# A four-layer graph network on one core: zero products between the first columns' sums, a column's blocks in another order, small loads later, and one held multiply that reads SBUF

## The chip, the core and the metric

The kernel runs on one core of a Trainium2 chip. The metric is the device time of one execution in microseconds (us). Before the change it is 2249.74 us, the median of three runs (2249.08 to 2251.6). The engines are named as in the profile: PE is TensorE (matmuls), PEld its weight loads, DVE is VectorE, ACT is ScalarE, POOL is GpSimd and SP is SyncE, whose queue issues the large loads.

## The reference, cut to what matters

The inputs are x (4096 x 128) and adj (4096 x 4096, sparse by value but stored dense, 64 MB). Each of four layers makes x = layernorm(x + layer(x, adj)).

```
layer 0:  hw = h @ W;  h_plus = (adj > 0) @ hw;  h_minus = (adj < 0) @ hw
          e_plus  = leaky_relu(h_plus @ a1 + h_minus @ a2)
          scores = where(adj > 0, e_plus, -9e15), and e_minus where adj < 0
          out = (softmax(scores, axis=1) * adj) @ hw
layer 1:  twice: Tx1 = L @ x; Tx2 = 2 (L @ Tx1) - Tx0
          h = elu(x @ W[0] + Tx1 @ W[1] + Tx2 @ W[2] + b)         (L = adj)
layer 2:  C = alpha_src[None] + alpha_dst[:, None];  tau = adj.T * exp(max(0.2 C, C))
          out = einsum(adj.T * tau / sum(tau), h_prime) + bias     (4 heads of 32)
layer 3:  out = h @ W_self + (adj @ h / clip(sum(adj, 1), 1)) @ W_neigh
```

## The kernel before, in words

The adjacency lies in HBM in two tilings, and every layer reads it again: blocks of 512 x 512 (1 MB, tile `chunk`, from in_adjT) and blocks of 256 x 1024 (also 1 MB, from in_adj). NB = 8 is the number of blocks in a column, P = 128, TB = 4 the tiles of 128 rows in a block, IB = 512. Five buffers named `chunk` (pool `ld`, bufs=5) take the loads, issued by SP in order.

**Layer 0** (L263 to L490) uses that adj has no negative entries; a flag (`bad`) checks it and would start a general version (L158) instead. It goes over the columns i = 0 to 7 (L383). In each it takes the eight blocks j in the order of L387 and L388. For each block VectorE makes a 0/1 mask `pos` (L308), TensorE adds four packed 32-column products of it into one PSUM tile `pden` (edge_sums, L345), and ScalarE runs through the block to look for negative entries (`junk`, L403). At the end of a column ScalarE copies the sums to SBUF (`parts`, L421), eight tiny products collect them (columns(), L352), VectorE and ScalarE make exp(e) from them (L423 to L427), and VectorE scales this column's rows of hw by it (L428). Only then can products with these rows run: product() (L357) of block j needs hw of column j, so in column i only the blocks j < i are multiplied at once. The diagonal block is multiplied in the next column, after its second block (diagonal(), L404). The blocks i+1 and i+2 stay in buffers of their own, three of each (`keep1`, `keep2`, pool l0k), and are multiplied three columns later by above() (L372). Blocks further up are loaded a second time (L459). Outside of the part named below a scheduler at compile time orders the instructions of each engine by priority, that is by place in the program, and by what it reckons to be ready. `keep_in_program_order` takes single instructions out of that.

28 products of a zeroed tile with itself (L317) run at the start, while the first loads are on their way. Nine small inputs for later layers are issued by ScalarE at the end of column 2 (later_inputs, L89), and at column 4 the tables made from them (later_constants, L96).

**Layer 1** (L523 to L582) is three passes of products over all 64 blocks; its last pass (L942 to L967) is interleaved by hand with layer 2.

**Layer 2** makes, for a tile of 128 source rows nt and two target blocks or one, `tau` and `tau2` on VectorE and GpSimd and multiplies them on TensorE (L755). A Pass is two target blocks by two heads (passes 0 to 5), or one block by four heads (passes 6 and 7); each has 32 steps, one per nt. A step of a wide pass is: ScalarE copies the row tile from `chunk` to a PSUM tile `a` (L705, which also sums the row); VectorE does two L733 and the first 704 columns of one more multiply (L737); GpSimd does the remaining columns (L738, L739). Passes 0 and 1 share each `a` and are stepped in pairs. While they run there is only one PSUM tile `a`; a second is opened when pass 0 is finished.

From L876 on (manual_schedule) the order on PE, DVE, ACT and POOL is the program's own. Small sequences are generators in the queue `chains`; one(chains) runs the next one to its next `yield`. These are block_end (L608, the end of layer 1 for a block), block_targets (L655, the table `dv` of a block), targets (L708, the tile D of a pass), finish (L764, the division at the end of a pass) and layer3_blocks (L782, the small products of layer 3). In the loop at L972 there are three calls per pair of steps while no layer-3 product is in `pieces`, and two otherwise. The layer-3 product (L813) is cut into pieces, one per matmul; a credit of 2.0 per pair of wide steps (3.4 for narrow ones) says how many run. It begins when the chain reaches start_product. PSUM tiles named `px`, `pp`, `den` and `num` are single buffers.

The softmax here doesn't subtract the row's maximum and nothing guards it: scores larger than these inputs give would overflow.

## Time and profile before

| Stretch, us | What runs | What is busy |
|---|---|---|
| 0 to 88 | layer 0, columns 0 to 2 | DMA 0.95, PE clock 0.81 |
| 88 to 330 | rest of layer 0 | PE 241.95 of 242 |
| 330 to 1090 | layer 1, three passes | PE 759.47 of 760 |
| 1090 to 1449 | layer 1's last pass, with passes 0 and 1 | PE 343.8 of 359 |
| 1449 to 1509 | end of passes 0 and 1 | DVE 45.27 of 60 |
| 1509 to 1947 | passes 2 to 5, layer-3 pieces | DVE 422, POOL 414 of 438 |
| 1947 to 2188 | passes 6 and 7, layer-3 pieces | PE 231, DVE 227 of 241 |
| 2188 to 2247 | end: last block's layer 3, output | PE 47.8 of 59 |

The page gives busy times in tenths for 40 slices of 56 us:

```profile
PE   6899999999999999999999999968999899999997
DVE  5544461000010110000025777779999999999995
PEclk8899999999999999999999999989999999999999
```

Slices 1 and 2 and slices 27 to 29 are those in which PE or its clock drops. A busy PE says only that matmuls were under way, not that it ran at its peak: in the pass stretches the count of matmuls and the waits tell more. In a line of the timeline the columns are the start in us, the duration in us, the engine, the line, the operation, the tiles written and read, the shape and the count, and in brackets the idle time of the engine just before it with what ended it.

### The profile page before, as it was taken

What the parts mean: (1) busy time and instruction counts of PE and PEld (TensorE: products, weight loads), DVE (VectorE), ACT (ScalarE), POOL (GpSimd) and SP (SyncE); (2) the same over time, 40 slices, a digit from 0 to 9 for tenths busy, and PEclk for the clock granted to TensorE, in tenths of its full rate; (3) what the DMA queues carried; (4) which work ended last, traced back from release to release, by engine and by line L of the source; (5) the groups of instructions that cost most, each with busy time, mean ns of one, the idle gap of its engine ahead of it and who ended that gap; (6) DMA issues with size and microseconds to landing.
All of it is one profiled execution on the core that took longest, in us unless ns stands there. A gap on an engine that the chain in (4) does not pass through costs nothing. (4 is left out here: it accounts for less than half of the span.)

```text
span 2247.5 us, 22889 instructions
## 1 busy us (share of the span) xinstructions
PE 2138.4 (95%) x8588; PEld 848.3 (38%) x8588; DVE 1174.6 (52%) x1815; ACT 561.9 (25%) x1016; POOL 854.4 (38%) x539
## 2 busy tenths in 40 slices
PE   6899999999999999999999999968999899999997
PEld 3344444444444444444443333312222222323334
DVE  5544461000010110000025777779999999999995
ACT  6654200000000000000032223234333433332213
POOL 0000000000000000000004766679999899989990
PEclk8899999999999999999999999989999999999999
DMA  9886748888767677778866556514666566645544
GB/s 397 312 301 214 243 168 283 301 302 300 268 237 259 232 243 262 262 264 272 283 228 232 199 196 235 206 57 165 242 231 238 194 244 243 219 140 204 187 169 170
DMA packets 87144, 528.17 MB, mean 235 GB/s; under 512 B 9328, under 2 KB 15472, under 8 KB 25712
## 3 DMA queue, kind: packets, MB, share of 16 engines
q1 hardware_dynamic: 78992, 521.31, 66.1%
q10 hardware_dynamic: 8032, 5.31, 0.8%
q8 instruction: 69, 1.13, 0.2%
q14 instruction: 51, 0.42, 0.1%
HBM read 524.49 MB, written 2.10 MB: 234 GB/s over the span
## 5 line engine op out<-in xcount | busy, mean ns | idle before, releaser
L733 DVE SCALAR_TENSOR_TENSOR tau<-D,es,a 128x1024 f32<-128x1024 f32 (+1 forms) x640 | 646.6, 1059 | 60.0 <-ACT a L705 34.7
L739 POOL TENSOR_TENSOR tau<-tau,chunk 128x1024 f32<-128x1024 f32 x192 | 456.0, 2375 | 14.4 <-DVE tau L733 13.6
L639 POOL TENSOR_TENSOR x<-x,B2R 128x512 f32<-128x512 f32 x8 | 10.2, 1275 | 1162.2 <-PE px L135 1162.2
L755 PE MATMUL num<-tau,hc 128*32 128x512 f32 x2048 | 325.2, 616 | 13.0 <-POOL tau L739 6.1
L755 PE MATMUL den<-tau,cs 128*32 128x512 f32 x2048 | 332.6, 605 | 4.4 <-DVE tau L733 3.0
L831 PE MATMUL pp<-chunk,xT 128*128 128x512 f32 (+1 forms) x488 | 231.6, 604 | 0.9 <-ACT D L721 0.9
L705 ACT ACTIVATE a<-chunk 128x1024 f32<-128x1024 f32 x160 | 164.3, 1027 | 245.0 <-DVE tau L737 206.1
L531 PE MATMUL pacc<-chunk,t 128*128 128x512 f32 x512 | 223.5, 592 | 0.0
L531 PE MATMUL pacc<-chunk,v 128*128 128x512 f32 x512 | 222.5, 592 | 0.0
L531 PE MATMUL pacc<-chunk,x 128*128 128x512 f32 x512 | 221.9, 593 | 0.0
L738 POOL TENSOR_TENSOR tau<-tau,chunk 128x320 f32<-128x320 f32 x192 | 167.2, 871 | 140.4 <-DVE tau L733 80.0
L955 PE MATMUL pp<-chunk,w 128*128 128x512 f32 x448 | 203.5, 598 | 0.8 <-DVE oT L615 0.8
L357 PE MATMUL pacc<-chunk,hw 128*128 128x512 f32 x408 | 195.1, 620 | 0.0
L737 DVE TENSOR_TENSOR tau<-tau,a 128x704 f32<-128x704 f32 x192 | 168.7, 878 | 0.0
L745 POOL TENSOR_TENSOR tau<-tau,chunk 128x1024 f32<-128x1024 f32 x64 | 151.9, 2373 | 1.1
L755 PEld LDWEIGHTS den<-tau,cs 128*32 128x32 f32 x2048 | 79.0, 112 | 179.5 <-issue 102.9
L755 PEld LDWEIGHTS num<-tau,hc 128*32 128x32 f32 x2048 | 60.8, 110 | 219.0 <-issue 115.4
L531 PEld LDWEIGHTS pacc<-chunk,v 128*128 128x128 f32 x512 | 97.2, 190 | 122.0 <-issue 122.0
L531 PEld LDWEIGHTS pacc<-chunk,x 128*128 128x128 f32 x512 | 96.4, 190 | 116.7 <-issue 116.7
L531 PEld LDWEIGHTS pacc<-chunk,t 128*128 128x128 f32 x512 | 96.1, 190 | 115.3 <-issue 115.3
L831 PEld LDWEIGHTS pp<-chunk,xT 128*128 128x128 f32 x488 | 85.7, 189 | 130.3 <-issue 127.6
L578 DVE COPY w<-ptr 128x512 f32<-128x512 f32 x8 | 5.5, 692 | 241.5 <-PE ptr L135 241.5
(215 smaller groups left out, 1668.1 us busy)
## 6 DMA issues: line engine op xcount, KB each, us to landing
chunk<-in_adjT SPq DMA_DIRECT2D x386, 1024.0 KB, 4.8
chunk<-in_adj SPq DMA_DIRECT2D x80, 1024.0 KB, 4.9
chunk<-in_adj SPq DMA_DIRECT2D x32, 512.0 KB, 4.7
keep<-in_adjT SPq DMA_DIRECT2D x13, 1024.0 KB, 7.2
xT<-in_xT ACTq DMA_DIRECT2D x8, 256.0 KB, 6.5
out<-o ACTq DMA_DIRECT2D x7, 256.0 KB, 2.3
W1A<-in_w1a ACTq DMA_DIRECT2D x1, 384.0 KB, 5.7
W1B<-in_w1b ACTq DMA_DIRECT2D x1, 384.0 KB, 6.5
```

Source lines behind the costliest of these rows:

```text
L357: nc.tensor.matmul(p, hw[:, j * TB + k, :], a[:, k, :], start=first and k == 0, stop=last and k == TB - 1)
L531: nc.tensor.matmul(p, stationary(c * TB + k), a[:, k, :], start=n == 0 and k == 0, stop=n == NB - 1 and k == TB - 1)
L639: nc.gpsimd.tensor_tensor(x[:, tb, :], x[:, tb, :], B2R[:, None, :].to_broadcast([P, TB, F]), ALU.add)
L705: nc.scalar.activation(ap, a, AF.Copy, accum_out=deg[:, nt, self.mp:self.mp + 1])
L733: nc.vector.scalar_tensor_tensor(flat(tau[:, q:q + n]), flat(self.D[:, q:q + n]), es[:, nt, head:head + 1], ap, op0=ALU.max, op1=ALU.mult)
L737: nc.vector.tensor_tensor(t2[:, 0:OWN], t[:, 0:OWN], ap[:, 0:OWN], ALU.mult)
L738: nc.gpsimd.tensor_tensor(t2[:, OWN:WB], t[:, OWN:WB], a[:, OWN:WB], ALU.mult)
L739: nc.gpsimd.tensor_tensor(t2[:, WB:2 * WB], t[:, WB:2 * WB], a, ALU.mult)
L745: nc.gpsimd.tensor_tensor(tau2[:, 2:4, :], tau[:, 2:4, :], rep(a, 2), ALU.mult)
L755: nc.tensor.matmul(acc[32 * q:32 * q + 32, :], weights(nt, head, is_den), r[:, q, :], start=nt == 0, stop=nt == NT - 1)
L831: nc.tensor.matmul(p, y[:, c * TB + k, :], a[:, k, lo:lo + n], start=c == blocks[0] and k == 0, stop=end)
L955: nc.tensor.matmul(p, w[:, c * TB + k, :], a[:, k, :], start=c == 0 and k == 0, stop=c == NB - 1 and k == TB - 1)
```

## The change

In layer 0, products of a zeroed weight tile (`nought`) with the mask just made are put on TensorE after each of the last four blocks of column 0 and each block of column 1. They keep TensorE at work while it waits for loads. The order of a column's blocks puts the two kept blocks ahead of block i-1, whose rows are scaled last. The small loads go to SP's queue at the end of column 5, the tables to column 7, and VectorE instead of ScalarE copies `parts` in the first four columns.

For the end of passes 0 and 1: the second multiply of a held pair (pass 1, after layer 1's last product) reads the row tile from SBUF instead of PSUM, so that `a` is free sooner. finish() does both of its transposes before it goes on, for passes 0, 1 and the last one, and layer3_blocks both halves of a block, for the first pair and the last block; the second PSUM tile for this is `pp` or `den`. Pass 3 gets its targets one at a time. block_targets of block 7 moves behind the start of the first layer-3 product.

The diff, cut to its core:

```diff
-            tc.keep_in_program_order(nc.scalar.dma_start(t, src))
+            tc.keep_in_program_order(nc.sync.dma_start(t, src))
...
+            nought = l0.tile([P, P], BF16, name="nought")
+            nc.vector.memset(nought, 0.0)
+            def keep_busy(moving, n):
+                idle = ps_tr.tile([P, IB], F32, name="ptr")
+                for k in range(n):
+                    nc.tensor.matmul(idle, nought, moving(k), start=True, stop=True)
+            keep_busy(lambda k: xp.rearrange("p t c -> p (t c)")[:, 0:IB], 28)
...
-                order = [*range(i + 3, NB), *range(i)]
-                order = order[:5] + list(range(i + 1, min(i + 3, NB))) + order[5:] + [i]
+                order = [*range(i + 3, NB), *range(i - 1), *range(i + 1, min(i + 3, NB)), *range(max(i - 1, 0), i + 1)]
...
                     edge_sums(pe, pos, j, both, n == 0, n == NB - 1)
+                    if i == 1 or i == 0 and n > 3:
+                        keep_busy(lambda k: pos[:, k, :], TB)
...
-                if i == 2:
+                if i == 5:
                     later_inputs()
+                if i == 7:
+                    later_constants(ps_mm, "pmm")
                 if i == 4:
-                    later_constants(ps_mm, "pmm")
...
-                nc.scalar.copy(parts, pe)
+                (nc.vector.tensor_copy if i < 4 else nc.scalar.copy)(parts, pe)
...
-                    size = 2 if self in passes[2:4] else 1
+                    size = 2 if self is passes[2] else 1
...
-                        nc.vector.tensor_tensor(t2[:, 0:OWN], t[:, 0:OWN], ap[:, 0:OWN], ALU.mult)
+                        only = self is passes[1] and layer1_done
+                        nc.vector.tensor_tensor(t2[:, 0:OWN], t[:, 0:OWN], (a if only else ap)[:, 0:OWN], ALU.mult)
...
-                    q = transpose4(ps_x, "px", lambda k: self.nd[:, 1, k * P:(k + 1) * P])
+                    more = (ps_p, "pp") if self in passes[0:2] else (ps_nd, "den") if self is passes[-1] else None
+                    turn = lambda pool, name, i: transpose4(pool, name, lambda k: self.nd[:, i, k * P:(k + 1) * P])
+                    q = turn(ps_x, "px", 1)
+                    if more:
+                        qn = turn(*more, 0)
                     yield
...
+                        pool, name = ((ps_nd, "den") if final else (ps_p, "pp") if blocks[0] == 0 else (ps_x, "px"))
+                        q = (pool if half else ps_x).tile([P, 2, 2, F], F32, name=name if half else "px")
...
+                        if half == 0 and (final or blocks[0] == 0):
+                            continue
                         yield
...
+                            if this is passes[1]:
+                                chains.append(block_targets(NB - 1))
...
-                            chains.append(block_targets(ib))
+                            if ib < NB - 1:
+                                chains.append(block_targets(ib))
...
                 load()
+                layer1_done.append(True)
```

## The prediction

> **What bounds the kernel now.** I read the table of windows by stage first, because the shares of the page average four layers with different limits. Its columns are the stretch in us, then its length, the busy time and count of each engine, the granted TensorE clock, the DMA share and GB/s.
>
> ```profile
> 0.00:88.00 88.00, 63.66 (x286) 30.38 (x286) 50.22 (x117) 58.90 (x66) 0.70 (x6) 0.81 0.95 375
> 88.00:330.00 242.00, 241.95 (x866) 103.94 (x862) 121.37 (x271) 89.51 (x107) 0.00 (x0) 0.99 0.68 236
> 330.00:1090.00 760.00, 759.47 (x1939) 346.86 (x1938) 59.11 (x128) 37.84 (x61) 0.00 (x0) 1.00 0.79 268
> 1449.00:1509.00 60.00, 41.93 (x235) 10.84 (x238) 45.27 (x56) 19.74 (x38) 40.32 (x26) 0.83 0.21 77
> 1509.00:1947.00 438.00, 408.73 (x2402) 120.88 (x2394) 422.24 (x437) 176.31 (x334) 414.07 (x267) 0.98 0.61 222
> ```
>
> From 88 to 1090 us TensorE is never free at full clock, so what makes its solid stretch begin earlier moves all that follows by the same amount. From 1509 on VectorE (422 of 438) and GpSimd (414) run in lockstep. The two holes are 0 to 88 us (clock 0.81, DMA 0.95) and 1449 to 1509 us (no engine over 45 of 60, DMA 0.21). The change edits both.
>
> The timeline shows the first hole's end: how column 2 of layer 0 closes and diagonal(2), the first product of the solid stretch, starts at 88.40.
>
> ```profile
> 78.76 0.83 PE L345 MATMUL pden<-pos,both 128*32 128x512 bf16 x12
> 81.37 0.59 ACT L421 COPY parts<-pden 128x512 f32<-128x512 f32 x1 [4.01 <-DMA W2S<-in_w2T]
> 81.53 0.14 DVE L104 COPY att<-ATS 32x1 f32<-32x1 f32 x1 [4.73 <-DMA ATS<-in_att_src]
> 82.01 1.87 PE L352 MATMUL ptr<-sel,parts 128*128 128x2 f32 x8 [2.41 <-ACT parts L421]
> 87.66 0.68 DVE L428 TENSOR_TENSOR hw<-hw,xe 128x512 f32<-128x512 f32 x1
> ```
>
> The sums end at 79.6, but their copy waits until ScalarE has issued nine small loads, VectorE stands 4.73 us on one of these loads, and TensorE's column sums run at half clock. At full clock the same sums take half:
>
> ```profile
> 111.28 0.95 PE L352 MATMUL ptr<-sel,parts 128*128 128x2 f32 x8
> ```
>
> The waits of 25 to 90 us name the other cost of the half clock: ScalarE, standing in order for a slow diagonal product, frees the load buffers late.
>
> ```profile
> ACT numT L364 <- PE pacc L357: 7.6, 2, 4.3
> DVE e L423 <- PE ptr L352: 9.2, 3, 5.6
> ```
>
> The second hole, in VectorE's timeline: block_targets(7) (L664, L667), then the next pair of steps, which starts only after ScalarE's copy L705.
>
> ```profile
> 1479.84 0.88 DVE L737 TENSOR_TENSOR tau<-tau,a 128x704 f32<-128x704 f32 x1
> 1480.00 2.38 POOL L739 TENSOR_TENSOR tau<-tau,chunk 128x1024 f32<-128x1024 f32 x1
> 1484.69 1.01 ACT L705 ACTIVATE a<-chunk 128x1024 f32<-128x1024 f32 x1
> 1486.01 2.47 DVE L733 SCALAR_TENSOR_TENSOR tau<-D,es,a 128x1024 f32<-128x1024 f32 x2 [1.83 <-ACT a L705]
> 1492.50 1.03 ACT L705 ACTIVATE a<-chunk 128x1024 f32<-128x1024 f32 x1 [6.58 <-DVE tau L737]
> 1493.73 2.47 DVE L733 SCALAR_TENSOR_TENSOR tau<-D,es,a 128x1024 f32<-128x1024 f32 x2 [1.27 <-issue]
> ```
>
> Here ScalarE's copy waits for the last reader of the one PSUM tile `a`, the L737 of the second step, and VectorE idles 1.27 us per pair.
>
> **What the Trainium skill says.** "TensorE: Matmul & The Clock Gate", section "What's actually happening": the array's clock is halved unless the recent activity window (about 3.4 us) was busy. The trace agrees: 0.50 from 30 to 40 us where TensorE works 4.9 of 10, and 1.87 against 0.95 us above. That products of zeros count is shown by the 28 of L317: 0.43 us apart at first, 0.21 us after 6.7 us. "SBUF — State Buffer", section "Who interferes with whom": a VectorE instruction with two SBUF inputs contends with a GpSimd one that reads SBUF, and the later one waits. No L737 of before has two SBUF inputs (`a` is PSUM), so no row shows it. "Trainium Kernel Development and Optimization", section "Key Constraints": issuing loads from another engine only saves the issuer's time. That fits: the loads cost ScalarE 75.36 to 81.33 us.
>
> **The change, part by part: layer 0.** (1) Zeros: 4 products after each of the last 4 blocks of column 0 and all 8 of column 1, 48 in all. At 0.21 us they are 0.86 us per block, 10 us; at half clock 1.7 us per block. A block lands each 2.5 us (1.05 MB at 421 GB/s) and column 1 holds 8 sums of 0.4, two products of 3.4 and 6.9 us of zeros: 17 of 20 us, so all of it lies beside the loads. Queued behind the zeros is the column sum (at most 0.86 us, beside the copy of 0.7). (2) With the clock up, diagonal(0) takes 3.4, not 5.9 us (it starts at 39.68), and ScalarE frees buffers 2 us sooner. (3) Order: for column 2, 5 6 7 0 3 4 1 2 in place of 5 6 7 0 1 3 4 2. The kept blocks have free buffers of their own, so the loads are no longer held at that point. In return the product of block i-1 (3.4 us) stands ahead of the last block's sums on TensorE, up to 1.5 us later than its landing would allow. (4) The nine loads leave ScalarE for SP at column 5, where DMA is 0.66 to 0.77 busy and TensorE is the bound: about 5 us of issue beside five loaded buffers, at nothing. The copies of later_constants move to column 7, where VectorE is half idle. (5) `parts` on VectorE: 0.69 us (the like copy of L548) instead of 0.56 on ScalarE; the masks queue behind it, but ScalarE's copy waited behind 1.91 us activations.
>
> Sum for column 2: the last block landed at 73.0 and should land at 70.5 to 72; sums by 73.5. Column 3 of the trace shows a close without disturbance: copy at 110.23, hw scaled at 115.57, 5.3 us. So hw is ready at 79 instead of 88.34. TensorE may still be cold for diagonal(2) (5.48 us now, no zeros in column 2). From then on the work is the same; I take off 1.5 us for blocks that then land too late (kept buffers that wait for above()). I take 8 us; bounds 2 (only the two waits on the small loads) and 11.
>
> **Layer 2 to 3.** (6) block_targets(7) leaves the hole: pair 28 to 29 took 1474.28 to 1486.01, 11.7 us. Two steps are 6.36 (2.47 + 0.88 less overlap, 3.18 each) plus 0.4 for a copy that starts early: 6.9. That is -4.9. Its instructions run later, among the steps: L664 and L667 (1.4 us) and the 1.23 us between them on VectorE, +2.6. (7) L737 of the second step reads `a` from SBUF: the copy starts 0.88 us earlier in three more pairs (7.7 us each). But GpSimd's L739, ready at the same moment, must now wait out L737: its pair becomes 2 x (0.87 + 2.37) + 0.88 = 7.4 us and replaces VectorE as the bound. I take 0.4 for each, -1.2 (bounds -2.6 and, if VectorE is the one that waits 2.4 us in each of six steps, +9). (8) finish() and layer3_blocks for the first pair do two transposes, or both halves, at a time: four calls of the chain fewer. At three calls per pair of steps the layer-3 product begins 1.3 pairs sooner (now 1552.9), while TensorE is idle (18.6 of 25 us busy at 1520 to 1545). With 2 pieces per pair, 2.7 pieces of 0.86 us leave the end, where leftover pieces still run at 2200.85 to 2204.3 although y is done by 2202.4: -2.3. The eight scalings in one go are 2 us on ScalarE beside its slack of 2.03 us per step: nothing. (9) Pass 3's targets one at a time: two more calls, due 60 us later: nothing. The last pass's wider finish: -0.3.
>
> Sum: -4.9 + 2.6 - 1.2 - 2.3 - 0.3 = -6.1. In all -14.1: 2249.7 - 14.1 = 2236.
>
> **Rivals.** A, the forecast, 0.50. B, layer 0 gives little: column 2's end stays set by landings, and the product ahead of the last sums eats what the loads gain: -3, with -6 from the rest, 2241. For it: DMA is at 1.01 until 55 us. Against: VectorE and ScalarE waits after the landing are most of the 15 us from 73.0 to 88.4. 0.17. C, the lock: VectorE or GpSimd loses in (7) what (6) gained, the rest -8 and -1: 2241. For it: L737 and L739 start 0.16 us apart. Against: L737 starts first in each pair. 0.15. D, slower: the zeros and the later product delay each early column, the masks wait behind `parts` in VectorE's order, layer 0 loses 4 us, and the lock costs 2.4 us in some steps: +5, 2255. For it: the order of layer 0's instructions is chosen ahead of the run, and no row shows the new one. 0.11. E, both holes close: -11 and -9, 2230. 0.07.
>
> **How the numbers follow.** 2236 is A's. The range of 2227 to 2247 holds A, B, C and most of E, and leaves D out. Within 0.2% is 2245.2 to 2254.2. A, E and most of B and C are faster: 0.81; 0.08 for the same; 0.11 slower.
>
> **What would show it.** TensorE's clock at or near 1.0 from 30 to 60 us; diagonal(2) at about 80; layer 1's first product at about 331 instead of 338.9; no L664 between 1440 and 1500 less the shift; the step after pair 28 following at 7 us; the first L831 about 20 us earlier (8 + 4 + 9, the last rounded up); no L831 of block 6 left when y is ready. It is wrong if diagonal(2) starts past 85, if L737 of the second step takes over 0.9 us, or if GpSimd's wait before L739 delays the next L733.

## The result and the profile after

The changed kernel takes 2245.41 us, median of four runs (2242.59 to 2247.08), against 2249.84 us for the kernel before (2249.08 to 2251.6): a ratio of 0.9978, 95% interval 0.9961 to 0.9995. The direction was forecast, the size was not: -4.4 us instead of -14.1, and the time lies in the upper part of the range. The profiled execution is the slowest of the four. Its span is 2245.2 us against 2247.5, so the differences that I follow through the two traces sum to -2.3 us.

Line numbers move by some 5 in layer 0 and by 9 or more later: L345 is now L350, L352 L357, L357 L362, L421 L430, L428 L437, L531 L540, L705 L714, L733 L742, L737 L748, L739 L750, L831 L853, L955 L980.

The table of windows of the kernel after, in the columns of the table before:

```profile
0.00:88.00 88.00, 71.87 (x334) 32.13 (x334) 52.46 (x122) 55.59 (x60) 0.70 (x6) 0.94 0.91 365
88.00:330.00 242.00, 240.93 (x867) 102.14 (x866) 123.23 (x277) 90.86 (x108) 0.00 (x0) 1.00 0.68 242
330.00:1090.00 760.00, 758.38 (x1932) 346.66 (x1931) 57.80 (x122) 37.81 (x61) 0.00 (x0) 1.00 0.78 267
1449.00:1509.00 60.00, 43.25 (x274) 12.66 (x272) 50.87 (x62) 20.57 (x41) 49.02 (x30) 0.89 0.27 93
1509.00:1947.00 438.00, 414.79 (x2376) 119.07 (x2380) 422.75 (x439) 179.60 (x338) 414.36 (x267) 0.99 0.62 223
```

Both holes look better filled: TensorE's clock is 0.94 instead of 0.81 in the first, and VectorE works 50.9 instead of 45.3 us in the second. But the row from 330 to 1090, which the change does not touch, has lost 1.1 us of TensorE's time. A table of busy shares says neither what the filling is worth nor why that row changed; for that I took the start of the same instruction in both traces.

| Start of | before | after | difference |
|---|---|---|---|
| diagonal(2), first L357 / L362 of it | 88.40 | 81.94 | -6.46 |
| last product of layer 0 | 336.98 | 335.45 | -1.53 |
| first product of layer 1 (L531 / L540) | 338.90 | 337.37 | -1.53 |
| last product of layer 1 | 1089.52 | 1090.65 | +1.13 |
| first product of layer 2's interleave (L955 / L980) | 1092.20 | 1094.17 | +1.97 |
| step after pair 28 (L733 / L742) | 1486.0 | 1483.7 | -2.3 |
| first step of pass 2 | 1509.2 | 1504.5 | -4.7 |
| 17th step of pass 2 | 1567.8 | 1566.7 | -1.1 |
| 97th step of passes 2 to 5 | 1841.9 | 1838.3 | -3.6 |
| first step of pass 6 | 1946.8 | 1943.2 | -3.6 |
| last step | 2185.2 | 2183.0 | -2.2 |

So of 6.5 us gained at diagonal(2) 4.9 are gone by the end of layer 0, and 3.5 more are lost at the two ends of layer 1. Layer 2 begins 2 us LATER than before, and all that the change brings is made after that point.

**The first hole.** The timeline after, at the end of column 2:

```profile
77.31 0.40 PE L350 MATMUL pden<-pos,both 128*32 128x512 bf16 x4
77.76 0.69 DVE L430 COPY parts<-pden 128x512 f32<-128x512 f32 x1 [5.47 <-PE pden L350]
78.51 1.05 PE L357 MATMUL ptr<-sel,parts 128*128 128x2 f32 x8 [0.80 <-DVE parts L430]
81.21 0.68 DVE L437 TENSOR_TENSOR hw<-hw,xe 128x512 f32<-128x512 f32 x1
81.94 5.18 PE L362 MATMUL pacc<-chunk,hw 128*128 128x512 f32 x6
```

The chain from the copy to hw takes 3.45 us instead of 6.29, the column sums run at full clock (1.05 against 1.87), but VectorE has stood 5.47 us in front of the copy, waiting for TensorE's last sums. The long waits of the same stretch answer to the two rows of before:

```profile
ACT numT L369 <- PE pacc L362: 7.9, 3, 4.2
DVE e L432 <- PE ptr L357: 2.3, 2, 1.1
```

The wait for the column sums is a quarter of what it was; that of ScalarE for the diagonal product has not moved.

**The second hole**, in the timeline after. The pair begins at 1476.80, the next one at 1483.72:

```profile
1479.18 0.88 DVE L748 TENSOR_TENSOR tau<-tau,a 128x704 f32<-128x704 f32 x1
1479.35 2.38 POOL L750 TENSOR_TENSOR tau<-tau,chunk 128x1024 f32<-128x1024 f32 x1 [0.33 <-DVE tau L742]
1482.37 0.94 DVE L748 TENSOR_TENSOR tau<-tau,chunk 128x704 f32<-128x704 f32 x1
1482.48 1.03 ACT L714 ACTIVATE a<-chunk 128x1024 f32<-128x1024 f32 x1 [6.12 <-DVE tau L742]
1482.53 3.02 POOL L750 TENSOR_TENSOR tau<-tau,chunk 128x1024 f32<-128x1024 f32 x1
1483.72 2.47 DVE L742 SCALAR_TENSOR_TENSOR tau<-D,es,a 128x1024 f32<-128x1024 f32 x2 [0.41 <-issue]
```

ScalarE's copy L714 starts beside the second L748 and no longer behind it, and the pair takes 6.9 us, exactly as forecast for this one pair. The three pairs after it take 6.9 us too, against 7.7 before.

**The start of layer 1.** This is where 2.66 us go. The timeline before, and then that after:

```profile
340.50 0.43 DVE L541 TENSOR_TENSOR wd<-W1B 128x256 f32<-128x256 f32 x1 [1.35 <-DMA W1B<-in_w1b]
344.85 0.49 PE L135 MATMUL ptr<-ident,x 128*128 128x128 f32 x2 [0.53 <-DVE x L149]
```

```profile
340.07 0.43 DVE L550 TENSOR_TENSOR wd<-W1B 128x256 f32<-128x256 f32 x1 [2.44 <-DMA W1B<-in_w1b]
344.41 0.50 PE L135 MATMUL ptr<-ident,x 128*128 128x128 f32 x2 [1.62 <-DVE x L149]
```

The load of the weights W1B landed at 340.48 before and at 340.04 after: it was issued 2.2 us earlier, beside a block of the adjacency with the DMA full (share 1.03 from 335 to 340), and came only 0.44 us earlier. VectorE's difference wd of these weights, which no product needs before 870 us, stands in its order ahead of the last normalization of layer 0; TensorE waits for the transposes that follow. After 1.62 us of waiting TensorE's clock falls to a half, as the windows after show (0.66 is the mean clock of the stretch):

```profile
340.00:345.00 5.00, 3.38 (x13) 1.52 (x12) 4.46 (x22) 0.30 (x1) 0.00 (x0) 1.00 0.73 252
345.00:350.00 5.00, 5.00 (x18) 3.04 (x18) 2.39 (x14) 0.58 (x1) 0.00 (x0) 0.66 0.05 21
```

Before, the wait of 0.53 us at this place left the clock at 1.00. The bill is 1.09 us of wait and 1.57 us of half clock. The second part need not come with every wait of this size: the last section shows longer waits that left the clock alone.

**The end of layer 1** costs 0.84 us more. Before, TensorE went on at once (L955 at 1092.20, no bracket); after, its first product for layer 2 waits for ScalarE's copy out of the PSUM pool of layer 1:

```profile
1094.17 5.42 PE L980 MATMUL pp<-chunk,w 128*128 128x512 f32 x12 [0.68 <-ACT xT L591]
```

### The profile page after: what moved, and what is told of

It reads as the page before. It is cut to its first block, busy times and chain, and to the rows that moved or that the text cites. A ratio compares the mean times of both kernels' runs of the same rounds, so it can differ in the third digit from the quotient of the medians.

```text
span 2245.2 us, 22994 instructions
## 1 busy us (share of the span) xinstructions
PE 2148.4 (96%) x8636; PEld 847.1 (38%) x8636; DVE 1178.2 (52%) x1820; ACT 562.1 (25%) x1014; POOL 857.3 (38%) x539
## 5 line engine op out<-in xcount | busy, mean ns | idle before, releaser
L742 DVE SCALAR_TENSOR_TENSOR tau<-D,es,a 128x1024 f32<-128x1024 f32 (+1 forms) x640 | 646.6, 1059 | 52.3 <-ACT a L714 32.0
L750 POOL TENSOR_TENSOR tau<-tau,chunk 128x1024 f32<-128x1024 f32 x192 | 459.1, 2391 | 12.7 <-DVE tau L742 12.0
L766 PE MATMUL num<-tau,hc 128*32 128x512 f32 x2048 | 332.7, 611 | 13.6 <-POOL tau L750 6.4
L766 PE MATMUL den<-tau,cs 128*32 128x512 f32 x2048 | 338.3, 601 | 2.0 <-DVE tau L742 0.4
L853 PE MATMUL pp<-chunk,xT 128*128 128x512 f32 (+1 forms) x488 | 231.7, 604 | 0.0
L714 ACT ACTIVATE a<-chunk 128x1024 f32<-128x1024 f32 x160 | 164.3, 1027 | 253.0 <-DVE tau L748 194.4
L540 PE MATMUL pacc<-chunk,t 128*128 128x512 f32 x512 | 223.5, 592 | 0.0
L540 PE MATMUL pacc<-chunk,x 128*128 128x512 f32 x512 | 223.1, 595 | 0.0
L540 PE MATMUL pacc<-chunk,v 128*128 128x512 f32 x512 | 222.5, 592 | 0.0
L980 PE MATMUL pp<-chunk,w 128*128 128x512 f32 x448 | 203.6, 598 | 1.5 <-DVE oT L624 0.8
L362 PE MATMUL pacc<-chunk,hw 128*128 128x512 f32 x408 | 194.0, 615 | 1.1 <-DVE hw L437 1.1
L748 DVE TENSOR_TENSOR tau<-tau,a 128x704 f32<-128x704 f32 x186 | 163.4, 879 | 0.0
L540 PEld LDWEIGHTS pacc<-chunk,v 128*128 128x128 f32 x512 | 97.2, 190 | 122.0 <-issue 122.0
L540 PEld LDWEIGHTS pacc<-chunk,x 128*128 128x128 f32 x512 | 96.7, 191 | 117.5 <-issue 117.4
L540 PEld LDWEIGHTS pacc<-chunk,t 128*128 128x128 f32 x512 | 96.1, 190 | 115.3 <-issue 115.3
L853 PEld LDWEIGHTS pp<-chunk,xT 128*128 128x128 f32 x488 | 85.7, 190 | 128.6 <-issue 125.8
```

Source lines behind the costliest of these rows:

```text
L362: nc.tensor.matmul(p, hw[:, j * TB + k, :], a[:, k, :], start=first and k == 0, stop=last and k == TB - 1)
L540: nc.tensor.matmul(p, stationary(c * TB + k), a[:, k, :], start=n == 0 and k == 0, stop=n == NB - 1 and k == TB - 1)
L714: nc.scalar.activation(ap, a, AF.Copy, accum_out=deg[:, nt, self.mp:self.mp + 1])
L742: nc.vector.scalar_tensor_tensor(flat(tau[:, q:q + n]), flat(self.D[:, q:q + n]), es[:, nt, head:head + 1], ap, op0=ALU.max, op1=ALU.mult)
L748: nc.vector.tensor_tensor(t2[:, 0:OWN], t[:, 0:OWN], (a if only else ap)[:, 0:OWN], ALU.mult)
L750: nc.gpsimd.tensor_tensor(t2[:, WB:2 * WB], t[:, WB:2 * WB], a, ALU.mult)
```

## The experiments

All were timed against the kernel before on the same chip. Times differ from run to run by more than most effects here: seven kernels with the same first layer (the change, e1, e3, e4, e10, e11, e12) scaled hw of column 2 at 79.0 to 81.9 us and began layer 1 at 334.5 to 338.1. So I judge each step by starts and waits inside a trace, one for each kernel, and the sum by the ratio. "Relative" means less the shift that the trace already has at layer 2's first product.

### Each half alone (e1, e2)

e1 is the kernel before with the hunks of layer 0 only, e2 that with the hunks of layers 2 and 3 only. Cut to one line for each hunk:

```diff
 # e1
+tc.keep_in_program_order(nc.sync.dma_start(t, src))        # at column 5; constants at column 7
+order = [*range(i + 3, NB), *range(i - 1), *range(i + 1, min(i + 3, NB)), *range(max(i - 1, 0), i + 1)]
+keep_busy(lambda k: pos[:, k, :], TB)
+(nc.vector.tensor_copy if i < 4 else nc.scalar.copy)(parts, pe)
 # e2
+only = self is passes[1] and layer1_done
+more = (ps_p, "pp") if self in passes[0:2] else (ps_nd, "den") if self is passes[-1] else None
+if this is passes[1]: chains.append(block_targets(NB - 1))
```

> The kernel before with the edits of the first layer alone. Theory S (seams): the earlier start of the solid stretch is mostly filled up again by TensorE's own work, so layer 1's first product stands 1.5 us earlier than before; then the wait of VectorE for W1B and the clock after it take 2.7 us, and a new wait of the first product of layer 2 for ScalarE takes 0.9 us. Layer 2 begins 2.1 us LATER than before, the end is 2251.9 (+2.1). Rival A (the forecast's sum with a smaller layer 0): the first layer's edits keep a gain of 1.5 to 2 us, 2248. Rival C (the two halves disturb each other): the first layer's edits alone bring the 8 us forecast, 2242.

> The kernel before with the edits of layers 2 and 3 alone. Theory S: layer 2 begins as before (first step 1194.5), the pair 28 to 29 takes 6.9 us, the three pairs after it 6.9 instead of 7.7, the moved block_targets(7) costs 2.6 later, and nothing is gained at the end: -4.4, 2245.4, as fast as the whole change. Rival A: these edits bring about 3 us and the first layer's about 1.5, 2247. Rival C: 2249 or more, since the head start of 8 us is needed for them.

e1: 2249.36 us, ratio 1.0002 (0.9994 to 1.0011). Diagonal(2) 6.9 us earlier, layer 1's first product 2.0 earlier, its last product 0.1 later, layer 2's first product 0.9 later, the end 1.1 later. TensorE's wait at 343 us was 1.06 instead of 1.62 us here; it lost 2.1 us at that place and 0.84 at the next, where 2.7 and 0.9 were expected. The time is 0.5 us above that of the kernel before, timed with it at 2248.9; theory S said 2.1 above, rival A 1.7 below, rival C some 8 below. That rules out C; between S and A it is the trace that decides, where the head start is used up at layer 1's last product. The first layer's edits alone bring nothing that can be measured.

e2: 2245.43 us, ratio 0.9988 (0.9981 to 0.9994). Layer 2 begins 0.2 us earlier than before, pass 2 7.1 earlier, the end is 4.3 earlier. Half of the change makes all of its gain.

### The wait for W1B (e3) and the one for ScalarE (e4)

```diff
-nc.vector.tensor_sub(wd, W1B[:, 0:HH, :], W1B[:, 2 * HH:3 * HH, :])
-nc.vector.tensor_scalar_mul(w2x, W1B[:, 2 * HH:3 * HH, :], 2.0)
+nc.gpsimd.tensor_tensor(wd, W1B[:, 0:HH, :], W1B[:, 2 * HH:3 * HH, :], ALU.subtract)
+nc.gpsimd.tensor_tensor(w2x, W1B[:, 2 * HH:3 * HH, :], W1B[:, 2 * HH:3 * HH, :], ALU.add)
```

```diff
-ph = ps_mm.tile([P, IB], F32, name="pmm")
+ph = (ps_acc if ib == NB - 1 else ps_mm).tile([P, IB], F32, name="pacc" if ib == NB - 1 else "pmm")
```

> The changed kernel, with wd and w2x made from W1B by GpSimd, which is idle there, instead of VectorE. Theory S: VectorE no longer stands 2.4 us on the load of W1B, TensorE's idle stretch of 1.62 us at 342.8 shrinks to 0.3 us or none, the clock stays at 1.0 from 345 to 350, layer 1 ends 2.7 us earlier than in the changed kernel, and the time is 2242.7. Rival T (throttle): the half clock there comes of the longer unbroken work of TensorE, not of its wait; it stays at 0.66 from 345 to 350, and the time is 2244.5 to 2245.4.

> As the run before, and the last of the products pmm that ScalarE copies to xT at the end of layer 1 is written to a buffer of ps_acc instead of ps_mm, so that the first product of layer 2 has no wait for ScalarE. Theory S: the first product of layer 2 follows at once, 0.9 us more, 2241.8. Rival D (the 0.9 us are needed anyway, for the load of the first block of layer 2 or for w): no difference to the run before, 2242.7.

e3: 2242.7 us, ratio 0.9974 (0.9964 to 0.9985). The windows of e3:

```profile
340.00:345.00 5.00, 5.00 (x25) 3.08 (x24) 2.32 (x11) 0.59 (x1) 0.02 (x1) 1.00 0.60 213
345.00:350.00 5.00, 5.00 (x16) 2.22 (x15) 2.97 (x16) 0.88 (x2) 0.00 (x0) 1.00 0.74 224
```

TensorE has no idle time and full clock. From layer 1's first product to its 33rd the trace gains 0.8 us on the kernel before, where the change lost 2.66. The throttle rival falls: the same amount of work, without the wait, kept its clock, and so did e4 to e15, which all have this edit. The time does not show the step by itself: the intervals of 0.9974 and 0.9978 overlap, and that 2242.7 is the number expected is in part luck, since the kernel before ran at 2248.9 beside it, 0.9 us faster than beside the change. That edit leaves the order of all other instructions of VectorE as it was, so I use e3 as the base of all that follows.

e4: the wait is gone; layer 1's last and layer 2's first product have the same shift (-1.54 each, against -3.32 and -2.48 in e3). Rival D is out for that place. But the run as a whole is not faster, 2244.29 us, ratio 0.9977 (0.9970 to 0.9984): its layer 0 ran 1.8 us later by the scatter named above, and at the last step only 2.8 us of the relative gain are left (e3: 3.6). 0.8 us is shown in the trace and not in the time. Why the wait appears with the edits of layer 0 and not without them (e2 has none) I did not find. The later kernels narrow it: e5 to e15 all have it (3.5 us from the last product of layer 1 to the first of layer 2, against 2.68 before and in e2), with or without the zeros, the new order or the moved loads. Of the edits of layer 0 only `parts` on VectorE is in all of these, and it was not taken out alone.

### The parts of layer 0 (e5 to e8)

All on top of e3. e5 leaves the zeros of columns 0 and 1 out (the 28 products at the start stay), e6 has the old order, e7 the small loads and constants where they were, and e8 has eight more products of zeros:

```diff
 # e5
-if i == 1 or i == 0 and n > 3:
-    keep_busy(lambda k: pos[:, k, :], TB)
 # e6
-order = [*range(i + 3, NB), *range(i - 1), *range(i + 1, min(i + 3, NB)), *range(max(i - 1, 0), i + 1)]
+order = [*range(i + 3, NB), *range(i)]
+order = order[:5] + list(range(i + 1, min(i + 3, NB))) + order[5:] + [i]
 # e7
-tc.keep_in_program_order(nc.sync.dma_start(t, src))
+tc.keep_in_program_order(nc.scalar.dma_start(t, src))
-if i == 5:
+if i == 2:
     later_inputs()
-if i == 7:
+if i == 4:
     later_constants(ps_mm, "pmm")
 # e8
 sums = columns(parts)
+if i == 2:
+    keep_busy(lambda k: pos[:, k % TB, :], 8)
```

> The kernel of the run with wd on GpSimd (2242.7, hw of column 2 at 80.8, first product of layer 1 at 336.35), without the products of zeros of columns 0 and 1. Theory Z (the clock is what brings column 2 early): hw of column 2 at 83 or later, clock 0.5 again from 30 to 40. Rival L (the small loads and the landings are): hw within 1 us of 80.8. For the end, theory F (the time saved at column 2 is filled up again, because TensorE's own sums move into the solid stretch): whatever hw does, layer 1 begins within 1.5 us of 336.35, 2242.7 to 2244; rival G (start decides): layer 1 shifts by as much as hw.

> The kernel of the run with wd on GpSimd, with the old order of a column's blocks. Theory F: hw of column 2 comes later (83 to 86), diagonal(2) with it, but TensorE then has done more sums ahead of it and fewer switches behind it, so that layer 1 begins within 1.5 us of 336.35: 2242 to 2244. Rival G: layer 1 shifts by as much as hw, 2 to 5 us: 2245 to 2248.

> The kernel of the run with wd on GpSimd, with the nine small loads back on ScalarE at column 2 and the copies of later_constants back at column 4. The forecast's step: hw of column 2 waits for ScalarE's issues and for a small load again, and comes at 86 to 87. Theory F: layer 1 begins 1 to 2 us later than 336.35, about 2244. Rival G: 5 to 6 us later, 2248. Rival N (the loads didn't matter): hw at 81, 2242.7.

> The kernel of the run with wd on GpSimd, and eight more products of zeros after the column sums of column 2, where TensorE stands 1.8 us and its clock falls to a half. Theory F: diagonal(2) runs at full clock, 3.7 instead of 5.2 us, and as TensorE is never free after it the whole 1.5 us arrive: 2241.2. Rival H (the loads that follow set the pace after diagonal(2)): a wait of the same size opens later in the layer, 2242.7. Rival I: the zeros stand ahead of the first sums of column 3 and put diagonal(2) off by 1 us or more, 2243.7.

| | hw of column 2 | diagonal(2) to the end of layer 0 | first product of layer 1 | time, us | ratio |
|---|---|---|---|---|---|
| before | 87.66 | 249.2 | 338.90 | 2249.68 | 1 |
| e3 | 80.83 | 253.4 | 336.35 | 2242.70 | 0.9974 (0.9964 to 0.9985) |
| e5 no zeros | 81.27 | 253.5 | 336.80 | 2242.74 | 0.9969 (0.9958 to 0.9981) |
| e6 old order | 78.29 | 253.4 | 333.81 | 2240.41 | 0.9958 (0.9941 to 0.9975) |
| e7 loads back | 82.57 | 250.1 | 334.69 | 2239.50 | 0.9961 (0.9947 to 0.9975) |
| e8 warm | 82.45 | 251.8 | 336.27 | 2240.72 | 0.9964 (0.9952 to 0.9977) |

**e5: with the new order the 48 zeros bring nothing.** Rival L holds: hw and the stretch behind it are as with them. Up to column 2's close the clock was a symptom and not the bound. Since the DMA is full there (share 1.01 to 1.02 from 20 to 50 us), I take the loads to set the pace. One thing did move: the last block of column 2 landed at 71.8 in e5, and at 70.4 to 71.1 in all the runs with the zeros. That is some 1 us, of which hw shows 0.4, because with the new order the sums come late anyway. What the zeros are worth with the old order was not tried.

**e6: the new order is a loss.** It was expected to be a gain ahead of diagonal(2); its removal is one of 2.5 us. The last block of column 2 lands at 70.9 us in both. The timeline after, then that of e6, from the mask of that block (L308) to the copy:

```profile
71.06 1.23 DVE L308 TENSOR_SCALAR pos<-chunk 128x2048 bf16<-128x2048 f32 x1 [1.26 <-DMA chunk<-in_adjT]
73.15 1.98 PE L362 MATMUL pacc<-chunk,hw 128*128 128x512 f32 x4
75.39 1.98 PE L362 MATMUL pacc<-chunk,hw 128*128 128x512 f32 x4
77.76 0.69 DVE L430 COPY parts<-pden 128x512 f32<-128x512 f32 x1 [5.47 <-PE pden L350]
```

```profile
71.00 1.23 DVE L308 TENSOR_SCALAR pos<-chunk 128x2048 bf16<-128x2048 f32 x1 [1.26 <-DMA chunk<-in_adjT]
71.41 2.84 PE L362 MATMUL pacc<-keep,hw 128*128 128x512 f32 x6
74.18 0.62 PE L350 MATMUL pden<-pos,both 128*32 128x512 bf16 x8
74.85 0.69 DVE L430 COPY parts<-pden 128x512 f32<-128x512 f32 x1 [2.62 <-PE pden L350]
```

With the new order the product of block i-1, in two parts of 1.98 us, stands on TensorE ahead of the last sums: VectorE waits 5.47 us, with the old order 2.62. The forecast saw this term and put it at "up to 1.5 us"; the earlier landing that should have paid for it is not there. The scatter is as large as the effect: the copy stands 4.8 to 7.9 us behind the landing with the new order (ten runs, mean 6.4), and 3.6 to 5.0 with the old one in e6, e9, e13 and e15, but 6.4 in e14. With all five the mean is 4.6, so the order costs about 2 us. Why e14 is late I did not trace; the small loads in ScalarE's queue are not the reason by themselves, since e9 has them there too.

**e7: the small loads do hold up column 2, and moving them is not free.** In e7's timeline ScalarE's exponential stands behind the last of its nine issues:

```profile
79.59 0.33 ACTq L94 DMA_DIRECT2D W<-in_w3s  x1
79.97 0.20 ACT L435 ACTIVATE xe<-xe 128x4 f32<-128x4 f32 x1 [4.99 <-DMA W2S<-in_w2T]
80.82 0.13 DVE L104 COPY att<-ATS 32x1 f32<-32x1 f32 x1
82.57 0.69 DVE L436 TENSOR_TENSOR hw<-hw,xe 128x512 f32<-128x512 f32 x1
```

hw is 1.7 us later, as expected in sign (3.4 to 4.4 us less than expected). Yet layer 1 begins 1.7 us EARLIER than in e3, which neither theory F nor G had: the stretch behind diagonal(2) is 3.4 us shorter. So theory F, that the gain is only filled up by TensorE's own sums, is not enough. What the stretch is made of can be counted in the traces. Behind diagonal(2)'s start there are always 464 matmuls of product(). The other terms are below; the column "half clock" says for how long TensorE's granted clock was 0.50 behind diagonal(2)'s start, and the last one takes half of that off the stretch.

| | groups of products | matmuls of sums | TensorE idle, us | half clock, us | stretch, us | at full clock, us |
|---|---|---|---|---|---|---|
| before | 58 | 280 | 0.05 | 3.6 | 249.2 | 247.4 |
| e9 | 60 | 288 | 0.05 | 5.2 | 251.0 | 248.4 |
| e7 | 61 | 288 | 0.05 | 2.8 | 250.1 | 248.7 |
| e14 | 62 | 288 | 1.07 | 3.2 | 251.7 | 250.1 |
| e15 | 63 | 292 | 3.52 | 6.8 | 257.0 | 253.6 |
| change | 66 | 292 | 1.07 | 4.8 | 254.1 | 251.7 |
| e3, e6 | 66 | 292 | 1.07 | 3.4 | 253.4 | 251.7 |
| e8, e13 | 66 | 292 | 1.07 | 0 | 251.8, 251.7 | 251.8, 251.7 |

The last column takes away what looked like scatter: every kernel with 66 groups needs 251.7 or 251.8 us, whatever its order and its zeros. The 0.7 us by which the change's stretch is longer than e3's are half clock.

The time between two matmuls shows what a group costs: product to product 0.43 us, product to sums 0.52, sums to product 0.31, and the second product of a group 0.53; sums that follow sums come in fours at 0.22. A group more costs 0.09 + 0.31 + 0.10, less the 0.22 that its sums would need behind other sums: an estimate of 0.28 us, and eight are 2.3. The idle time at column 3's close is 1.0. Twelve matmuls of sums, three fours or 0.7 us, are work that TensorE did before in its hole, ahead of diagonal(2), and does now behind it. That is 4.0 of the 4.3 us at full clock; the rest I have not traced. The same sum gives e9, e7 and e14 to within 0.1 us (1.0, 1.3 and 2.6 for 1.0, 1.3 and 2.7) and leaves 0.7 us of e15's 6.2 open. "From then on the work is the same" was wrong twice.

**e8: a warm diagonal(2) is worth 1.7 us.** Its stretch is 251.8 instead of 253.4, and the half clock behind diagonal(2) is gone, 3.4 us of it in e3. The run shows no gain at layer 1's start because its column 2 closed 1.6 us later, before the added zeros come into play; e13 settles it.

### Putting the parts together (e9, e13 to e15)

e9 combines e6 and e7. e13 is e3 with the old order, e8's zeros, and layer 3's calls one at a time again (see e12). e14 and e15, both with the old order, take the moved inputs apart:

```diff
 # e14, on e6
-tc.keep_in_program_order(nc.sync.dma_start(t, src))
+tc.keep_in_program_order(nc.scalar.dma_start(t, src))
-if i == 5:
+if i == 2:
     later_inputs()
 # e15, on e6
-tc.keep_in_program_order(nc.sync.dma_start(t, src))
+tc.keep_in_program_order(nc.scalar.dma_start(t, src))
```

> The kernel of the run with wd on GpSimd, with both the old order of a column's blocks and the small inputs back at column 2 (constants at column 4); zeros, parts on VectorE and the edits of layers 2 and 3 stay. Theory K: the order costs 2.5 us ahead of diagonal(2), in TensorE's own order, and the moved inputs cost some 3.5 us behind it, in more switches between products and sums (66 groups of products; this kernel has 60) and one idle stretch. The two are apart, so they add: hw of column 2 at 80 (78.3 + 1.7), the stretch from diagonal(2) to the last product 249 to 249.5 us, first product of layer 1 at 331.5 to 332, 2237 to 2238. Rival M (both come from the same landings): no better than the faster of the two alone, 2239.5 to 2240.5.

> The kernel of the run with wd on GpSimd, with the old order of blocks, eight more products of zeros behind the column sums of column 2, and finish() and layer3_blocks one at a time again. Theory K2: column 2 closes within 4 us of the landing of its last block, diagonal(2) at 79 at full clock, the stretch behind it 251.8 instead of 253.4, first product of layer 1 at 332.2; the step of 8.0 to 9.5 us at 1965 to 1974 is one of 6.0 again; in sum 2237 to 2238.5. Rival M2 (what is saved ahead is lost in later waits): 2240 to 2242.

> The kernel of the run with wd on GpSimd and the old order, with the nine small loads back on ScalarE at column 2 and the constants left at column 7. If the loads' place at column 5 made the stretch behind diagonal(2) longer: 250 to 251 us, and as VectorE has no copy of a small load at column 4, hw of column 2 at 79 to 80: layer 1 at 331 to 332, 2238. If the constants at column 7 did: 253 or more, 2241.

> The kernel of the run with wd on GpSimd and the old order, with the nine small loads at column 5 as in the change, but issued by ScalarE. If SyncE's queue (nine issues ahead of the chunks) made the stretch longer: 250 to 251 us, layer 1 at 330 to 331, 2238. If it is the place in TensorE's order that the loads and constants shift (63 groups of products here, 66 with SyncE): about 252, 2239. If the constants at column 7: 253.4, 2240.4 as with SyncE.

e9: 2242.15 us, ratio 0.9962 (0.9948 to 0.9976), and theory K falls. The parts do not add. `parts` was copied at 74.5, as early as in e6, but hw came at 83.45: with the sums early, the whole wait for the small loads stands open, 8.9 us from copy to hw instead of 3.4. The stretch was 251.0, 1.5 us longer than expected: TensorE waited so long for hw that 5.2 us behind diagonal(2) ran at half clock, against 2.8 in e7. At full clock e9's stretch is the shortest of all the kernels with moved edits, 248.4. So the forecast's step on the small loads was right with the old order (5.5 us), and 1.7 us in e7 because the late sums hid the rest.

e13: 2237.36 us, ratio 0.9950 (0.9936 to 0.9963), 12.6 us faster than before and, by times or by ratios, 8 or 6 faster than the change. Column 2 closed 5.0 us behind the landing (4 expected), diagonal(2) at 80.09 (79 expected), the stretch behind it 251.7 (251.8 expected), layer 1 at 333.16 (332.2 expected), and the time as expected. The timeline of e13:

```profile
77.57 1.89 PE L320 MATMUL ptr<-pos,nought 128*128 128x512 bf16 x7
80.09 2.84 PE L362 MATMUL pacc<-chunk,hw 128*128 128x512 f32 x6 [0.20 <-DVE hw L439]
```

The six matmuls take 2.84 us; after the change they took 5.18. Here the zeros are worth something: TensorE is about to run without a break, and there is no load to hide the cold clock behind.

e14: 2242.53 us, ratio 0.9970 (0.9959 to 0.9981); hw at 82.87, because ScalarE's exponential again waits behind the nine issues, stretch 251.7 with 1.02 us of idle time at 174.6. e15: 2244.35 us, ratio 0.9978 (0.9967 to 0.9988); hw at 77.9, the earliest of all, but a stretch of 257.0, with 3.5 us of idle time, 2.25 of it in one piece at 171.9 where TensorE waits for a mask of VectorE. None of the three expectations for e15 fits: SyncE's queue is not what made the stretch longer, for without it the stretch is worse. At full clock, all with the old order, the stretch is 248.4 with loads and constants where they were (e9), 250.1 with the constants at column 7 (e14), 251.7 with the loads on SyncE at column 5 as well (e6), and 253.6 with these on ScalarE (e15). So the constants' move costs 1.7 us, of which 1.0 is the idle time, and the loads' move 1.6 more, one trace each. Each place gives another order of TensorE's and VectorE's instructions, and with it another count of groups and of waits; why the scheduler chooses these orders stays open.

### The parts of layers 2 and 3 (e10 to e12)

All on top of e3. e10 has L748 read PSUM in every step again, e11 has block_targets(7) back behind the last block, e12 undoes the paired calls of finish() and layer3_blocks (cut to its core):

```diff
 # e10
-nc.vector.tensor_tensor(t2[:, 0:OWN], t[:, 0:OWN], (a if only else ap)[:, 0:OWN], ALU.mult)
+nc.vector.tensor_tensor(t2[:, 0:OWN], t[:, 0:OWN], ap[:, 0:OWN], ALU.mult)
 # e11
-if this is passes[1]:
-    chains.append(block_targets(NB - 1))
-if ib < NB - 1:
-    chains.append(block_targets(ib))
+chains.append(block_targets(ib))
 # e12
-q = turn(ps_x, "px", 1)
-if more:
-    qn = turn(*more, 0)
+q = transpose4(ps_x, "px", lambda k: self.nd[:, 1, k * P:(k + 1) * P])
...
-if half == 0 and (final or blocks[0] == 0):
-    continue
```

> The kernel of the run with wd on GpSimd, with the held pairs' multiply by a (128x704) reading PSUM in every step again. Theory B (the copy of the next pair waits for nothing but that multiply; the lock of VectorE and GpSimd on SBUF costs nothing): the three pairs after the first moved one take 7.7 instead of 6.9 us, step 64 stands 2.4 us later (1502.7), and all of it arrives at the end: 2245. The forecast's size: 1.2 us, 2243.9. Rival Q (given back later, in the lockstep of passes 2 and 3): 2242.7.

> The kernel of the run with wd on GpSimd, with block_targets(7) back behind the last block of layer 2. Theory B and the forecast agree: the pair 28 to 29 takes 11.7 less the 0.8 of the SBUF copy again, 4.8 us more at step 58, of which 2.6 come back where it now runs in passes 2 and 3: 2244.9. Rival Q (the later cost is as large as the gain): 2242.7.

> The kernel of the run with wd on GpSimd, with finish() and layer3_blocks taking one transpose and one half at a time again (and the last pass's wider finish undone). The forecast's step: the product of layer 3 begins some 8 us later, and 2 to 2.7 of its pieces move to the end, 2.3 us, with the last finish 2.6: 2245.3. Theory E (the queue of pieces runs empty between two pairs of blocks, so a head start is lost in that gap): the first product of layer 3 some 8 us later, the gap after its 128th matmul shorter by as much, the end within 0.5 us: 2242.7, and 0.3 for the last finish.

e10: 2246.48 us, ratio 0.9986 (0.9980 to 0.9993), against 0.9974 for e3. In its timeline ScalarE's copy is behind the multiply again, and VectorE waits 1.27 us per pair:

```profile
1483.92 0.88 DVE L746 TENSOR_TENSOR tau<-tau,a 128x704 f32<-128x704 f32 x1
1484.83 1.03 ACT L714 ACTIVATE a<-chunk 128x1024 f32<-128x1024 f32 x1 [6.57 <-DVE tau L746]
1486.07 2.47 DVE L742 SCALAR_TENSOR_TENSOR tau<-D,es,a 128x1024 f32<-128x1024 f32 x2 [1.27 <-issue]
```

The pairs take 7.7 us, pass 2 begins 2.8 us later relative to e3, and at the first step of pass 6 it is 3.2. Theory B holds up to there: more than twice the forecast's 1.2 us. At the last step 1.4 are left, because of one stall: at the 17th step of pass 6 some traces wait 2 us longer than others (the step takes 5.9 us in e3 to e6, e9, e14 and e15, and 3.9 in the change, e2, e7, e8, e10 and e11), which moves the end by some 1.7 us. So a difference of that size at the end says little about an edit.

e11: 2241.48 us, ratio 0.9966 (0.9955 to 0.9978): not slower than e3. Relative to layer 2's start the pair 28 to 29 costs 4.1 us more (4.8 in the expectation); 2.7 are back by the 17th step of pass 2, as the forecast said; but 1.0 more comes back between the 65th and the 97th step of passes 2 to 5, and 0.5 stays at the first step of pass 6. That e11 ends up ahead is the stall just named. Rival Q: the move is right in its mechanism, and worth 0.5 us at most at the end.

e12: 2242.19 us, ratio 0.9970 (0.9958 to 0.9982). The layer-3 product begins 7.7 us later than in e3 (9.6 relative), and nothing is lost by it: in the profiled run the end is 2.6 us earlier than e3's relative to layer 2's start, while the times of e12 and e3 are the same within their intervals. So the forecast's gain is not there. The head start dies in a gap: the product of the first two blocks runs out of pieces before y of the next two is ready. The windows of its matmuls alone (busy time and count on PE and PEld, clock, DMA share, GB/s), before and then after:

```profile
1770.00:1780.00 10.00, 0.00 (x0) 0.00 (x0) 0.83 0.41 154
```

```profile
1750.00:1760.00 10.00, 0.53 (x2) 0.00 (x0) 1.00 0.57 211
1760.00:1770.00 10.00, 0.00 (x0) 0.00 (x0) 0.83 0.61 211
```

Between the 128th and the 129th of these matmuls lie 19.4 us before, 24.6 after, 18.0 in e12. And there is a price, at the seventh step of pass 6. In the timeline after, then in that of e12, VectorE's accumulation of a finished piece:

```profile
1969.08 1.88 PE L853 MATMUL pp<-chunk,xT 128*128 128x512 f32 x4
1971.00 0.69 DVE L862 TENSOR_TENSOR acc<-pp,acc 128x512 f32<-128x512 f32 x1 [3.39 <-PE pp L853]
```

```profile
1960.43 1.02 PE L842 MATMUL pp<-chunk,xT 128*128 128x512 f32 x2
1961.70 0.68 DVE L851 TENSOR_TENSOR acc<-pp,acc 128x512 f32<-128x512 f32 x1
```

With the head start the last pieces of a group fall into that step, four matmuls instead of two stand on TensorE ahead of the accumulation, and the step takes 9.5 us (8.0 in the kernels with e3's edit), before and in e12 and e13 6.0. Part of this comes back in the traces where the stall at the 17th step is missing: that step takes 6.1 us before and 3.9 after. Over eleven traces with the paired calls and all other edits of layers 2 and 3 (the change, e2 to e9, e14 and e15) the relative gain at the last step was 2.8 to 5.6 us, and without the pairs 6.6 (e12) and 6.0 (e13).

## Why the prediction was right or wrong

**Layer 0, -8: the step that failed.** At layer 2's first product it was +2.0 instead. Of the 10 us between them 2.9 were lost ahead of diagonal(2), 3.4 in the stretch behind it, and 3.5 at the two ends of layer 1. Taken apart:

- The close of column 2. hw was to be ready at 79 and was at 81.9 (its scaling started at 81.21; at 79.0 to 81.9 in the runs with this first layer). That the waits on the small loads would go was right, and so was the landing (70.9 against 70.5 to 72). The close took 4.1 us instead of 5.3. The last sums, due by 73.5, ran at 77.3. That is in the main item (3), the product ahead of the last sums, mis-sized at 1.5 us; e6 gives about 2.5.
- "At nothing" for the new place of the loads and "VectorE is half idle" for that of the constants: the stretch behind diagonal(2) is 3.4 us longer with both there (e7), 3.0 at full clock.
- "From then on the work is the same; I take off 1.5 us": 4.9 us, by 8 more groups of products, 12 matmuls of sums that had been done in the old hole, 1.0 us idle, and 0.6 of half clock. This is largely the item before, seen from the other side.
- Zeros, clock: the sign that I named came (1.00 from 30 to 40), the benefit did not: some 1 us at the landing, 0.4 at hw (e5). I had counted on it for a stretch that the loads set; and ScalarE's wait for the diagonal product, which I had put down to the half clock, is 7.9 us after and was 7.6 before.
- Not in the sum at all: the waits at both ends of layer 1, +2.66 and +0.84. I assumed that a shift passes through a full stretch unchanged. At its first seam, where layer 0 ends and layer 1 begins, stands a load whose landing did not shift with it. The Trainium skill, "TensorE: Matmul & The Clock Gate", section "What's actually happening", which I had used for the first hole, gives the clock's fall after an idle window of about 3.4 us; here 1.62 us of waiting sufficed, and 1.06 us in e1, while before 0.53 us did not.

What stands in place of -8 is -1.5 at layer 1's first product and +2.0 at layer 2's.

**Layers 2 and 3, -6.1: two thirds of it came, -4.2 at the last step of the profiled run, from terms that partly missed.** That the sum is near is in part luck: one term was too small, one did not come, and the stall at the 17th step of pass 6 moves the end by 1.7. block_targets(7): -4.8 for -4.9 and +2.7 for +2.6 (e11), but of the remaining 2 only 0.5 is left at pass 6. L737 from SBUF: -2.4 for -1.2. My reason for halving it came in part: GpSimd did wait, 0.63 us per pair for the 0.88 that I took, and worked without a break, but its pair took 6.97 us and not 7.4, against 6.92 on VectorE, so that it fell behind by 0.04 us per pair and held nothing up. The paired calls: for -2.3 no gain, and 2.0 us more at one step of pass 6 (e12, e13); the step "2.7 pieces leave the end" overlooked that the queue of pieces runs dry between two pairs of blocks, which the gap of 19.4 us before already showed. The last finish: 62.3 us from the start of the last step to the end before and 62.2 after, so nothing to be seen of -0.3. `parts` on VectorE and pass 3's targets were not tried alone.

**Rivals.** B, layer 0 gives little because the product ahead of the last sums eats what the loads gain, is nearest to what happened: it named item (3), and its 2241 was 4 us too low for the seams that it did not know. C, the lock, is out as a loss: GpSimd waits, but the next L742 starts on time. D's line that the order of layer 0's instructions is chosen ahead of the run and that no row shows the new one deserved more than 0.11: it is where the loss of the stretch lies.

**The signs.** Met: the clock, no block_targets in the hole, the pair of 6.9 us. Missed: layer 1's first product (337.4 for 331), the layer-3 product (14.2 us earlier for 20), no piece of block 6 left when y is ready (pieces still run at 2197.6 and 2198.4). The three tests that I gave for "wrong" would not have caught it; one did strike, L737 of the second step over 0.9 us (0.94 to 1.04), and meant nothing.

## What to carry to other kernels

A stretch in which an engine is never idle need not hand on what is gained ahead of it: count whether work moves from the old hole into it, and how often the engine changes between kinds of work. Then look at the first wait behind each seam: a load or a copy that does not shift with the rest takes the gain back, and more if the clock falls with it. And before speeding up the head of a queue, look whether the queue runs dry later.

## What the hardware showed that I had not expected

- VectorE with two SBUF inputs beside GpSimd cost GpSimd time, but the profile shows it as a longer instruction and not as a wait before it. The Trainium skill, "SBUF — State Buffer", section "Who interferes with whom", calls the shared port an exclusive lock; the numbers come near that: L748 took 0.94 to 1.04 us instead of 0.88 and the L750 that overlapped it 3.00 to 3.03 instead of 2.38, in each of the three pairs that I looked at. GpSimd, which starts 0.16 to 0.24 us after VectorE, pays 0.63 us and VectorE 0.06 to 0.16, together about the 0.8 us for which both overlap; for the pair it is harmless, since VectorE goes on.
- The length of a wait does not decide alone whether TensorE's clock falls. Waits of 1.62 us (at 343) and, in e1, of 1.06 halved it. But the same wait of 2.20 us, between the same instructions of pass 3, left it at 1.00 in the change and halved it in e3. The change first, then e3:

```profile
1644.99 0.38 PE L727 MATMUL px<-dv,selD 96*128 96x512 bf16 x1 [2.20 <-ACT D L730]
1645.00:1650.00 5.00, 5.00 (x37) 1.56 (x37) 5.00 (x5) 3.21 (x6) 3.84 (x4) 1.00 0.72 305
```

```profile
1640.85 0.38 PE L727 MATMUL px<-dv,selD 96*128 96x512 bf16 x1 [2.20 <-ACT D L730]
1642.30:1645.60 3.30, 3.30 (x20) 0.87 (x16) 3.30 (x4) 1.17 (x3) 3.04 (x3) 0.50 0.61 258
```

- In every trace of this case the spells of half clock last 3.41 us or a multiple of it (only the last one, at the end of the program, is cut short), and their starts lie on one grid of 3.41 us through the whole trace. Where a wait falls on that grid differs from trace to trace. In the change one spell begins at 79.9 us, 0.3 us into a wait of 1.78, so that wait did not start it. The half clock at the start of layer 1 is in the traces of both kernels that have the wait there, the change and e1; that every execution pays it is not shown.
- A switch between two kinds of matmul costs time that the profile books as busy: 0.53 instead of 0.43 us for the second product of each group, and 0.52 for the last. Eight more such groups are 2.3 us of 250 in which TensorE counts as busy throughout.
